# Two graph layers on one core: the hooks between the matmuls moved, merged and opened to ScalarE

## The chip, the cores and the metric

The kernel runs on one core of a Trainium2 chip. The metric is the device time of one execution in microseconds (us); lower is better. Everything is float32.

## The reference

128 graphs of 64 nodes with 768 features pass two layers, each followed by a residual and a layer norm. Cut to what matters:

```python
# layer 0, h = x
u = h @ h.T / sqrt(768);  p = softmax(u);  delta = p * adj
attn = delta / (sum(delta) + 1e-10)
ctx = upper(attn) @ (h @ Wl.T + bl) + diag(attn) * (h @ Ws.T + bs) + lower(attn) @ (h @ Wr.T + br)
x = layernorm(h + relu(layernorm(ctx) * gamma + beta))
# layer 1, 12 heads of 64
q, k, v = heads(x @ Wq + bq), heads(x @ Wk + bk), heads(x @ Wv + bv)
s = where(adj > 0, q @ k.T / 8 + abeta * adj, -9e15)
x = layernorm(x + softmax(s) @ v)
```

## The kernel before

**Blocks and periods.** The 8192 tokens are 16 blocks of 512 (8 graphs, four tiles `t` of 128 tokens). After a prologue that does layer 0 of block 0 and most of block 1's, the loop over `n` runs 16 periods. Period n holds, in this order of TensorE's large work: `left`, `right` and `own` (the three weight products wl, wr, ws of layer 0 for block m = n+1), `val` (the product wv of layer 1 for block n), and `qk[0]`, `qk[1]`, `qk[2]` (q and k of block n, one group of heads each). Period 0 has no `left`, `right` and `own`, and the last has no layer 0 at all, so 14 periods are whole. The attention of block p = n-1 is finished in `left` and `right` of period n.

**Seven products at 14 places.** Every large product is done by `seven` (L250) with seven block products instead of eight, in the order 1, 2, 6, 5, 7, 4, 3, each for two halves j. That makes 14 *places*, numbered 2k+j for the k-th product of the order. Products 1, 6, 7, 4 accumulate in the two PSUM tiles X[0], X[1], products 2, 5 and 3 use Y[0], Y[1]. Behind product 1, 6 and 7 `first` copies X with the bias to `u` (VectorE L297, or ScalarE L520 as `uqk` in the q/k products); `last` writes the outputs (L409 into `lr` for wl and wr, L391 into `o` for ws, L499 into `v` for wv, L528 into q and k). A later product can't go on in X or Y before those reads are done. In the trace one float32 matmul stands as two records, so a place of three matmuls is "x6".

**Hooks.** Small work is put ahead of a place by hand: `at(left, 4, f)` runs f ahead of place 4 of that stage (`hooks`, L259). The functions that the change moves:

- `turned_weights` (L572) transposes softmax weights by TensorE into the PSUM tile `ps_e` (pool `ps_tr`, two buffers, shared with `ps_a`), ScalarE copies to `eT`; `scores` (L533), `weighted` (L586) and `finish` (L611: layer norm and output of block p) are the rest of attention.
- `sides` (L372) transposes layer 0's attention through `ps_a` to `aT`; `context0` (L414) multiplies it with `lr` at the places of `val` (tile `ps_ctx`, pool `ps_mm` with two buffers) and puts the two norms, the affine step and the residual in the queue; the last step `norm` also stores x to DRAM as `x1d` (L447, by GpSimd's queue), because a block is loaded back in 32 x 32 squares:
- `squares` (L195) loads the tile `sq` (one buffer, 128-byte rows, four DMAs by ScalarE's queue, L201), from `x1d` for layer 1's input or from the input x for the next block's layer 0. `turned` (L205) transposes it on VectorE in six steps (L210) to `xT` or `hT`, and `combined` (L217) makes the sums S1, S2, S4 on GpSimd, four operations (L222 to L225). `begin1`, `turn1`, `sums1` are these three for layer 1, `begin`, `turn0`, `sums0` for layer 0, where `sums0` also runs `attention0` (matmuls `u`, L330).
- `loads` (L303) loads the plain tiles `xa` for the residual, by SyncE's queue, which also loads all weight pieces (pool `wst`, four buffers).

**Two queues of steps.** What VectorE and ScalarE do between is put by `later` in two lists, `urgent` and `lazy`. `step` (L119) runs behind every place and takes one item, from `urgent` first. An item marked `act` (an exponential or a square root on ScalarE) runs only where `act_free` is true and doesn't use up the step; a `GAP` leaves one step's room for the result. `settle(key)` (L130) runs all items of a kind at once. In q/k products `act_free` is false at most places:

```python
step(not taps_by_act or (j == 0 and i in (2, 5, 3)))
```

The loop runs under a manual schedule: each engine's instructions stand in the order in which this code issues them, and each engine goes through its own list in order. ScalarE's, SyncE's and GpSimd's DMAs stand in those lists too.

Of the kernel before, what the change touches and what calls it, by code (L numbers as in the profile page):

```python
# [11 lines left out]
F32 = mybir.dt.float32  # L12
AF = mybir.ActivationFunctionType
ALU = mybir.AluOpType
# [3 lines left out]
P = 128  # L18
# [5 lines left out]
T = 4  # L24
# [20 lines left out]
def gnn_two_layers(ctx: ExitStack, tc, x, adj, wl, bl, ws, bs, wr, br, gamma, beta,  # L45
# [204 lines left out]
    def seven(width, factors, first, last, hooks, taps_by_act=False):  # L250

        X, Y, u = {}, {}, {}
        for k, i in enumerate(ORDER):
            for j in range(2):
                for f in hooks.get(2 * k + j, ()):  # L259
                    f()  # L260
                if i == 1:
                    X[j] = ps_st.tile([P, 512], F32, tag="X", name="ps_X")
                if i in (2, 5):
                    Y[j] = ps_st.tile([P, 512], F32, tag="Y", name="ps_Y")
                ps = (X if i in (1, 6, 7, 4) else Y)[j][:, 0:width]
                fs = factors(i, j)
                for c, (a, b) in enumerate(fs):
                    nc.tensor.matmul(ps, lhsT=a, rhs=b, start=(c == 0 and i in (1, 2, 5)), stop=(c == len(fs) - 1),  # L268
                                     skip_group_check=True)
                if i == 1:  # L270
                    u[j, 1] = first(j, 0, ps)
                elif i == 2:
                    last(j, 0, 0, ps, u[j, 1])
                elif i == 6:
                    u[j, 2] = first(j, 1, ps)
                elif i == 7:
                    u[j, 3] = first(j, 1, ps)
                    last(j, 1, 1, Y[j][:, 0:width], u[j, 3])
                elif i == 4:
                    last(j, 1, 0, ps, None)  # L280
                elif i == 3:
                    last(j, 0, 1, ps, u[j, 2])
                step(not taps_by_act or (j == 0 and i in (2, 5, 3)))

    def by_tokens(nm, S, last, in_sbuf=None, hooks={}):

# [127 lines left out]
    def context0(n):  # L414

        blk = blocks[n]
        xa, o, dg = blk["xa"], blk["x"], blk["dg"]

        def part(t, h):
            cols = slice(h * HALF, (h + 1) * HALF)  # L420
            ps = ps_mm.tile([P, 512], F32, tag="mm", name="ps_ctx")
            for g in range(2):
                nc.tensor.matmul(ps[g * L : (g + 1) * L, 0:HALF], lhsT=blk["aT"][:, t, g * L : (g + 1) * L],  # L423
                                 rhs=blk["lr"][t][:, g, cols], start=True, stop=True)
            nc.vector.scalar_tensor_tensor(o[t][:, cols], o[t][:, cols], dg[:, t : t + 1], ps[:, 0:HALF],  # L425
                                           ALU.mult, ALU.add)
            if (t, h) == (T - 1, 1):
                rest()

        key = ("o", n)  # L430

        def affine(t, mean, rstd):
            nc.vector.scalar_tensor_tensor(o[t], o[t], mean, affine_of["gamma"], ALU.subtract, ALU.mult)

        def affine2(t, mean, rstd):
            nc.vector.scalar_tensor_tensor(o[t], o[t], rstd, affine_of["beta"], ALU.mult, ALU.add)

        def residual(t):
            nc.vector.scalar_tensor_tensor(o[t], o[t], 0.0, xa[t], ALU.max, ALU.add)

        squared = 0 < n < NBLK - 1
        blk["x_d"] = x_d = tc.dram_tile([NTOK, D], F32, name=f"x1d_{n}") if squared else None

        def norm(t, mean, rstd):
            nc.vector.tensor_scalar(o[t], o[t], mean, rstd, ALU.subtract, ALU.mult)  # L445
            if squared:
                nc.gpsimd.dma_start(out=x_d[t * P : (t + 1) * P, :], in_=o[t])  # L447

        def rest():
            for t, mr in enumerate(moments(key, o, 1e-12)):  # L450
                later(key, partial(affine, t, *mr), partial(affine2, t, *mr), partial(residual, t))
            for t, mr in enumerate(moments(key, o, 1e-5)):
                later(key, partial(norm, t, *mr))

        return [partial(part, t, h) for t in range(T) for h in range(2)]


    def transposed1(n):
# [110 lines left out]
              lambda: nc.vector.tensor_tensor(s8, s8, per_row(rz), ALU.mult), queue=urgent)  # L569
        blk[hg] = s  # L570

    def turned_weights(n, hg, t0, pool=None):  # L572

        blk = blocks[n]
        settle(("s", n, hg))
        e = blk[hg]
        if t0 == 0:
            blk["eT", hg] = (pool or l1_p).tile([P, T, 2, P], F32, tag="lr" if pool else "eT", name="eT")
        eT = blk["eT", hg]
        ps = ps_tr.tile([P, 4, P], F32, tag="tr", name="ps_e")  # L580
        for t in range(2):
            for c in range(2):
                nc.tensor.transpose(ps[:, 2 * t + c, :], e[:, t0 + t, c].rearrange("p r m -> p (r m)"), ident)
        nc.scalar.copy(eT[:, t0 : t0 + 2].rearrange("p t c i -> p (t c) i"), ps)

    def weighted(n, hg, tiles=range(T)):  # L586

# [95 lines left out]
    for n in range(NBLK):  # L683
# [4 lines left out]
        def at(hooks, place, f, *args):  # L688
            hooks.setdefault(place, []).append(partial(f, *args))

        def spread(hooks, place, fs):
            for k, f in enumerate(fs):
                at(hooks, place + k, f)
# [2 lines left out]
        last = n == NBLK - 1  # L696
        if p >= 0:
            one, two, three = (left, left, right) if not last else (qk[0], qk[1], qk[1])
            at(one, 2, turned_weights, p, 1, 0)
            at(one, 1 if not last else 2, scores, p, 2)  # L700
            at(one, 3, turned_weights, p, 1, 2)
            at(one, 5, weighted, p, 1)
            for k in range(2):
                at(two, 11 + k if not last else 1 + 2 * k, turned_weights, p, 2, 2 * k)
            at(two, 13 if not last else 5, weighted, p, 2)
            at(three, 0 if not last else 6, finish, p)

        if not last:
            if n > 0:
                if m + 1 < NBLK:  # L710
                    at(left, 4, edges, m + 1)
                at(right, 2, sides, m)
                sq1 = {}

                def begin1():
                    settle(("o", n))
                    blocks[n]["sq1"], sq1["fs"] = squares(blocks[n]["x_d"])

                at(right, 4, begin1)
                fetch = {}  # L720

                def begin2():
                    fetch["fs"] = loads(m)

                at(right, 8, begin2)
                for t in range(T):
                    at(right, 8 + t, lambda t=t: fetch["fs"][t]())
                for a in range(P // Q):
                    at(right, 4 + a, lambda a=a: sq1["fs"][a]())
                at(own, 0, settle, ("f", p))  # L730

                def turn1():
                    blocks[n]["xT"] = turned(("t1", n), blocks[n]["sq1"], f"xT_{n}")
                    later(("m", n), *mask(n), queue=urgent)

                at(own, 2, turn1)

                def sums1():
                    settle(("t1", n))
                    blocks[n]["S"] = combined(blocks[n]["xT"])  # L740

                at(own, 9, sums1)
                if m + 1 < NBLK:
                    sq = {}

                    def begin():
                        blocks[m + 1]["sq"], sq["fs"] = squares(x_b[m + 1])

                    at(own, 10, begin)
                    for a in range(P // Q):  # L750
                        at(own, 10 + a, lambda a=a: sq["fs"][a]())
                side_part(m, "l", None, left)
                side_part(m, "r", None, right)
                self_part(m, None, own)
            spread(val, 1, context0(m))
            if m + 1 < NBLK:

                def turn0():
                    blocks[m + 1]["hT"] = turned(("t", m + 1), blocks[m + 1]["sq"], f"hT_{m + 1}")

                at(val, 7, turn0)

                def sums0():
                    settle(("t", m + 1))
                    attention0(m + 1)

                at(qk[0], 2, sums0)

        if not last:
            values(n, val)  # L770
# [4 lines left out]
        at(qk[1], 2, scores, n, 0)  # L775
        at(qk[2], 2, scores, n, 1)
        if not last:
            for k in range(2):
                at(qk[2], 1 + 2 * k, turned_weights, n, 0, 2 * k)
            at(qk[2], 5, weighted, n, 0)  # L780
        for hg in range(NHG):
            projected(n, hg, qk[hg])
# [2 lines left out]

    for t0 in (0, 2):
        for hg in range(NHG):
            turned_weights(n, hg, t0, l0t if hg else None)
        for hg in range(NHG):
            weighted(n, hg, range(t0, t0 + 2))  # L790
            settle(("y", n, hg))
        finish(n, range(t0, t0 + 2))
        settle(("f", n))
# [31 lines left out]
```

## Time and profile before

| | |
|---|---|
| time, median of 3 runs | 3141.28 us (3139.05 to 3143.47) |
| the profiled execution | 3140.72 us, its span 3139.0 us |
| TensorE busy | 3022.5 us (96%) |
| VectorE, ScalarE, GpSimd busy | 2180.1, 398.3, 343.3 us |
| DMA | 541.20 MB, 172 GB/s over the span; the queue of `sq` moves 44.05 MB in 347568 packets |
| `left` of period 3 to `left` of period 4 | 711.07 to 903.64, 192.57 us |

How to read the views: a row of the timeline has the start in us, the duration, the engine, the line and operation, the tiles written and read, the shape, the count of merged records, and in brackets how long the engine stood idle before it and what released it. PE is TensorE, PEld its weight loads, DVE VectorE, ACT ScalarE, POOL GpSimd, SP SyncE; a "q" behind the name is the engine's sequencer, which issues DMAs. In the list of waits the columns are who waited for whom, us in total, times, and the longest.

### The profile page before, as it was taken

The page shows a single profiled execution, that of the slowest core. Times are in us where ns is not written, and L with a number is a line of the kernel's source. Part 1 is how long each engine was busy: PE and PEld are TensorE (multiplying, and loading weights), DVE is VectorE, ACT ScalarE, POOL GpSimd, SP SyncE. Part 2 cuts the span into 40 slices and gives each one's busy share as a digit, 9 for nine tenths or more (in the row PEclk, how much of TensorE's full clock was granted, in tenths as well). Part 3 has the DMA queues.
Part 4 walks back from the last instruction along what each step waited for, and adds up shares of the span by engine and source line. Part 5 has one row for each costly group of instructions (what it writes and reads, how often), then busy time and mean ns, then how long its engine had stood idle before and what let it go on. Part 6 is the DMA issues. An engine that isn't in the chain of part 4 may idle for free.

```text
span 3139.0 us, 45071 instructions
## 1 busy us (share of the span) xinstructions
PE 3022.5 (96%) x18144; PEld 2010.8 (64%) x18144; DVE 2180.1 (69%) x4163; ACT 398.3 (13%) x689; POOL 343.3 (11%) x317
## 2 busy tenths in 40 slices
PE   8899999999999999999999999999999999999997
PEld 5457657575674856758566585665757657575685
DVE  5747767677675866858667676676767767676756
ACT  0001102020020201102011020110201102020031
POOL 2321010100101001010100101001010010100010
PEclk9999999999999999999999999999999999999998
DMA  7663764937649475584755848568494764947343
GB/s 283 215 221 116 197 157 148 229 119 218 141 157 213 137 208 137 174 193 139 213 136 185 173 138 217 133 186 176 143 229 124 206 154 148 223 125 219 122 126 119
DMA packets 547791, 541.20 MB, mean 172 GB/s; under 512 B 372641, under 2 KB 452129, under 8 KB 547585
## 3 DMA queue, kind: packets, MB, share of 16 engines
q1 hardware_dynamic: 185424, 429.38, 43.9%
q10 hardware_dynamic: 347568, 44.05, 12.5%
q0 software_dynamic: 14592, 64.89, 5.5%
q8 instruction: 145, 2.38, 0.3%
q14 instruction: 62, 0.50, 0.1%
HBM read 473.37 MB, written 64.88 MB: 171 GB/s over the span
## 4 chain that ended last, share of the span: by engine, by line
issue 49%; PE 31%; DVE 8%; DMA 6%; POOL 4%; ACTq 2%; ACT 0%; POOLq 0%; SPq 0%; DVEq 0%
PE ps_X L268 15%; PE ps_Y L268 11%; DVE v L499 3%; PE ps_ctx L423 3%; DMA x1d<-o 3%; DVE hT L210 2%; ACTq L201 2%; DMA sq<-in_x_dram 1%; DVE u L297 1%; PE u L330 1%; POOL S L225 1%; POOL S L224 1%; POOL hT L223 1%; POOL x1d L447 1%; DMA sq<-x1d 1%
## 5 line engine op out<-in xcount | busy, mean ns | idle before, releaser
L268 PE MATMUL ps_X<-xT,wqk 128*128 128x256 f32 x1728 | 391.3, 379 | 0.0
L268 PEld LDWEIGHTS ps_X<-xT,wqk 128*128 128x128 f32 x1728 | 326.9, 190 | 47.0
L268 PE MATMUL ps_Y<-S,wqk 128*128 128x256 f32 x1152 | 264.3, 379 | 0.0
L268 PE MATMUL ps_X<-wr,hT 128*128 128x384 f32 x540 | 208.4, 542 | 53.5 <-DVE u L297 53.5
L409 DVE TENSOR_TENSOR lr<-ps_Y,u 64x384 f32<-64x384 f32 x384 | 213.2, 555 | 59.5 <-PE ps_Y L268 51.7
L268 PEld LDWEIGHTS ps_Y<-S,wqk 128*128 128x128 f32 x1152 | 218.9, 190 | 29.8
L520 ACT ACTIVATE uqk<-ps_X,bq 128x256 f32<-128x256 f32 x144 | 68.1, 473 | 1321.1 <-PE ps_X L268 1321.1
L268 PEld LDWEIGHTS ps_X<-wr,hT 128*128 128x128 f32 x540 | 113.1, 212 | 143.6 <-DVE u L297 64.9
L268 PE MATMUL ps_X<-wv,xT 128*128 128x384 f32 x576 | 200.2, 494 | 0.3
L238 DVE BATCH_NORM_STATS2 stats<-o 128x6 f32<-128x384 f32 x384 | 192.8, 543 | 1.4
L268 PE MATMUL ps_X<-ws,hT 128*128 128x384 f32 x540 | 184.7, 494 | 8.6 <-DMA ws<-d_s 5.4
L268 PE MATMUL ps_X<-wl,hT 128*128 128x384 f32 x540 | 188.3, 495 | 3.8 <-DVE std L243 2.7
L447 POOL DMA_DIRECT2D x1d<-o x56 | 30.5, 546 | 1333.2 <-DVE o L445 1318.1
L499 DVE TENSOR_TENSOR v<-ps_Y,u 64x192 f32<-64x192 f32 x384 | 136.4, 355 | 41.5 <-PE ps_Y L268 35.2
L268 PEld LDWEIGHTS ps_X<-wv,xT 128*128 128x128 f32 x576 | 105.4, 190 | 90.1 <-DVE u L297 17.4
L268 PEld LDWEIGHTS ps_X<-ws,hT 128*128 128x128 f32 x540 | 102.5, 192 | 84.6 <-DVE u L297 10.4
L528 DVE TENSOR_TENSOR q<-ps_Y,uqk 128x256 f32<-128x256 f32 x144 | 60.7, 421 | 133.2 <-ACT uqk L520 82.8
L268 PEld LDWEIGHTS ps_X<-wl,hT 128*128 128x128 f32 x540 | 101.7, 193 | 68.1 <-issue 4.4
L268 PE MATMUL ps_Y<-xT,wqk 128*128 128x256 f32 x576 | 140.2, 388 | 1.4 <-issue 1.4
L268 PE MATMUL ps_X<-S,wqk 128*128 128x256 f32 x576 | 136.7, 382 | 0.0
L268 PE MATMUL ps_Y<-wv,S 128*128 128x384 f32 x384 | 134.6, 494 | 0.0
L425 DVE SCALAR_TENSOR_TENSOR o<-o,dg,ps_ctx 128x384 f32<-128x384 f32 x128 | 78.5, 614 | 74.4 <-PE ps_ctx L423 73.3
(183 smaller groups left out, 4601.6 us busy)
## 6 DMA issues: line engine op xcount, KB each, us to landing
wqk<-qk_d SPq DMA_DIRECT2D x336, 384.0 KB, 3.0
wv<-d_v SPq DMA_DIRECT2D x64, 576.0 KB, 6.6
ws<-d_s SPq DMA_DIRECT2D x60, 576.0 KB, 6.3
wl<-d_l SPq DMA_DIRECT2D x60, 576.0 KB, 3.7
wr<-d_r SPq DMA_DIRECT2D x60, 576.0 KB, 4.0
wv<-in_L_gnn_Wv_dram SPq DMA_DIRECT2D x48, 576.0 KB, 4.2
ws<-in_L_gnn_W_self_dram SPq DMA_DIRECT2D x45, 576.0 KB, 4.8
wl<-in_L_gnn_W_left_dram SPq DMA_DIRECT2D x45, 576.0 KB, 3.9
```

What stands on the lines that cost most here:

```text
L201: nc.scalar.dma_start(out=sq[a * Q : (a + 1) * Q].rearrange("p s c i -> p (s c) i"), in_=by_group[a])
L210: nc.vector.transpose(xT[:, c, :].rearrange("p (j s) -> p s j", s=SQ), sq[:, :, c, :])
L223: nc.gpsimd.tensor_tensor(a21, a11, a21, ALU.subtract)
L238: nc.vector.bn_stats(stats[:, h, :], tiles[t][:, h * HALF : (h + 1) * HALF])
L268: nc.tensor.matmul(ps, lhsT=a, rhs=b, start=(c == 0 and i in (1, 2, 5)), stop=(c == len(fs) - 1), skip_group_check=True)
L409: nc.vector.tensor_tensor(lr[t][half * L : (half + 1) * L, g, cols], ps[rows], bias[nm][rows, cols] if part is None else part[rows], ALU.add)
L423: nc.tensor.matmul(ps[g * L : (g + 1) * L, 0:HALF], lhsT=blk["aT"][:, t, g * L : (g + 1) * L], rhs=blk["lr"][t][:, g, cols], start=True, s ...
L425: nc.vector.scalar_tensor_tensor(o[t][:, cols], o[t][:, cols], dg[:, t : t + 1], ps[:, 0:HALF], ALU.mult, ALU.add)
L447: nc.gpsimd.dma_start(out=x_d[t * P : (t + 1) * P, :], in_=o[t])
L499: nc.vector.tensor_tensor(v[r * L : (r + 1) * L, t, g, h * 3 : (h + 1) * 3, :], pairs(ps)[rows, r], add[rows, r], ALU.add)
L520: nc.scalar.activation(u, ps, AF.Identity, bias=bias["qk"[j]][:, c : c + 1])
L528: nc.vector.tensor_tensor(dst, ps, part, ALU.add)
```

## The change

- **Loads of layer 1's squares:** `begin1` and its four loads go from place 4 of `right` to place 10, so behind the square root of `finish` in ScalarE's list. `turn1` goes from place 2 of `own` to 4, `sums1` from 9 to 12. The next block's squares (`begin`) go from `own` 10 to `val` 0, `turn0` from `val` 7 to 8, `sums0` from `qk[0]` 2 to 4. The plain loads of x (`begin2`) go from `right` 8 to 11 to `own` 0 to 3. `sides` goes from `right` 2 to `left` 11.
- **Small work together:** `turned_weights` does both pairs of tiles at one place (three times a period), mostly beside `scores` or `sides`; `context0` does both halves of a tile at one place, so four places of `val` (1, 3, 5, 7) instead of eight. Small work then stands at 12 places per period instead of 22.
- **ScalarE's steps:** in q/k products an `act` item may run behind every place but two.

```diff
-                step(not taps_by_act or (j == 0 and i in (2, 5, 3)))
+                step(not taps_by_act or (i, j) not in ((5, 1), (7, 0)))
...
-        def part(t, h):
...
-            if (t, h) == (T - 1, 1):
+        def part(t):
+            for h in range(2):
+                cols = slice(h * HALF, (h + 1) * HALF)
+                ps = ps_mm.tile([P, 512], F32, tag="mm", name="ps_ctx")
+                for g in range(2):
+                    nc.tensor.matmul(ps[g * L : (g + 1) * L, 0:HALF], lhsT=blk["aT"][:, t, g * L : (g + 1) * L],
+                                     rhs=blk["lr"][t][:, g, cols], start=True, stop=True)
+                nc.vector.scalar_tensor_tensor(o[t][:, cols], o[t][:, cols], dg[:, t : t + 1], ps[:, 0:HALF],
+                                               ALU.mult, ALU.add)
+            if t == T - 1:
                 rest()
...
-        return [partial(part, t, h) for t in range(T) for h in range(2)]
+        return [partial(part, t) for t in range(T)]
...
-    def turned_weights(n, hg, t0, pool=None):
+    def turned_weights(n, hg, tiles=range(T), pool=None):
...
+        for t0 in tiles[::2]:
+            ps = ps_tr.tile([P, 4, P], F32, tag="tr", name="ps_e")
+            for t in range(2):
+                for c in range(2):
+                    nc.tensor.transpose(ps[:, 2 * t + c, :], e[:, t0 + t, c].rearrange("p r m -> p (r m)"), ident)
+            nc.scalar.copy(eT[:, t0 : t0 + 2].rearrange("p t c i -> p (t c) i"), ps)
...
-            at(one, 2, turned_weights, p, 1, 0)
             at(one, 1 if not last else 2, scores, p, 2)
-            at(one, 3, turned_weights, p, 1, 2)
+            at(one, 1 if not last else 2, turned_weights, p, 1)
             at(one, 5, weighted, p, 1)
-            for k in range(2):
-                at(two, 11 + k if not last else 1 + 2 * k, turned_weights, p, 2, 2 * k)
+            at(two, 11 if not last else 2, turned_weights, p, 2)
...
-                at(right, 2, sides, m)
+                at(left, 11, sides, m)
...
-                at(right, 4, begin1)
+                at(right, 10, begin1)
...
-                at(right, 8, begin2)
+                at(own, 0, begin2)
                 for t in range(T):
-                    at(right, 8 + t, lambda t=t: fetch["fs"][t]())
+                    at(own, t, lambda t=t: fetch["fs"][t]())
                 for a in range(P // Q):
-                    at(right, 4 + a, lambda a=a: sq1["fs"][a]())
+                    at(right, 10 + a, lambda a=a: sq1["fs"][a]())
...
-                at(own, 2, turn1)
+                at(own, 4, turn1)
...
-                at(own, 9, sums1)
+                at(own, 12, sums1)
...
-                    at(own, 10, begin)
+                    at(val, 0, begin)
                     for a in range(P // Q):
-                        at(own, 10 + a, lambda a=a: sq["fs"][a]())
+                        at(val, a, lambda a=a: sq["fs"][a]())
...
-            spread(val, 1, context0(m))
+            for t, f in enumerate(context0(m)):
+                at(val, 1 + 2 * t, f)
...
-                at(val, 7, turn0)
+                at(val, 8, turn0)
...
-                at(qk[0], 2, sums0)
+                at(qk[0], 4, sums0)
...
-            for k in range(2):
-                at(qk[2], 1 + 2 * k, turned_weights, n, 0, 2 * k)
+            at(qk[2], 2, turned_weights, n, 0)
```

More of the change, by code (lines that the diff above doesn't have):

```diff
@@ L417, in context0 @@
         xa, o, dg = blk["xa"], blk["x"], blk["dg"]
-        def part(t, h):
[L420 to L426, printed above, removed]
-            if (t, h) == (T - 1, 1):
+        def part(t):
[8 more added lines that the diff above has]
+            if t == T - 1:
                 rest()
@@ L576, in turned_weights @@
         e = blk[hg]
-        if t0 == 0:
+        if 0 in tiles:
             blk["eT", hg] = (pool or l1_p).tile([P, T, 2, P], F32, tag="lr" if pool else "eT", name="eT")
         eT = blk["eT", hg]
[L580 to L584, printed above, removed]
+        for t0 in tiles[::2]:
[4 more added lines that the diff above has]
+            nc.scalar.copy(eT[:, t0 : t0 + 2].rearrange("p t c i -> p (t c) i"), ps)
     def weighted(n, hg, tiles=range(T)):
@@ L787, in gnn_two_layers @@
         for hg in range(NHG):
-            turned_weights(n, hg, t0, l0t if hg else None)
+            turned_weights(n, hg, range(t0, t0 + 2), l0t if hg else None)
         for hg in range(NHG):
```

## The prediction

> **What bounds the kernel now.** I read the page's busy shares first, then the list of who waited for whom, then the timeline of one period (711.07 to 903.64 us, the one that starts layer 0 of block 4), TensorE alone and then all engines.
>
> ```profile
> PE 3022.5 (96%) x18144; PEld 2010.8 (64%) x18144; DVE 2180.1 (69%) x4163; ACT 398.3 (13%) x689; POOL 343.3 (11%) x317
> ```
>
> TensorE sets the time. Only what stops it, or what shortens its own work, counts. Its waits:
>
> ```profile
> PE ps_X L268 <- DVE u L297: 60.3, 21, 7.1
> PE u L330 <- DVE hT L210: 11.6, 14, 0.8
> ```
>
> Columns: total us, times, longest. The timeline shows where they fall (start, us, engine, line, operation; in brackets the idle time before it):
>
> ```profile
> 759.70 4.03 PE L268 MATMUL ps_X<-wr,hT 128*128 128x384 f32 x12
> 766.81 5.83 PE L268 MATMUL ps_X<-wr,hT 128*128 128x384 f32 x12 [3.08 <-DVE u L297]
> 772.48 4.03 PE L268 MATMUL ps_Y<-wr,S 128*128 128x384 f32 x12
> ...
> 791.83 5.97 PE L268 MATMUL ps_X<-ws,hT 128*128 128x384 f32 x18
> 799.17 2.20 PE L268 MATMUL ps_X<-ws,hT 128*128 128x384 f32 x6 [1.38 <-DVE u L297]
> 801.21 4.03 PE L268 MATMUL ps_Y<-ws,S 128*128 128x384 f32 x12
> ```
>
> Twelve records (two places) start 3.87 us apart when nothing disturbs, 1.935 a place. The four places from 759.70 to 772.48 should take 7.74 and take 12.78: 5.04 lost, of which 3.08 stand in brackets; the 12 records behind the wait are stretched to 5.67. The same four places in `right` over all 14 periods lose 82.8 us (3.9 to 9.4 each), the four in `own` 6.0. Why is `u` late?
>
> ```profile
> 758.00 0.17 DVE L243 TENSOR_SCALAR std<-mv 128x4 f32<-128x4 f32 x1
> 762.26 3.59 ACTq L201 DMA_DIRECT2D sq<-x1d  x2
> 765.89 0.20 ACT L246 ACTIVATE std<-std 128x4 f32<-128x4 f32 x1 [26.49 <-DMA ws<-in_L_gnn_W_self_dram]
> 766.13 0.18 DVE L247 RECIPROCAL rstd<-std 128x4 f32<-128x4 f32 x1 [7.50 <-ACT std L246]
> 766.23 0.53 DVE L297 TENSOR_TENSOR u<-ps_X,br 128x384 f32<-128x384 f32 x1
> ```
>
> The variance is ready at 758.17, but ScalarE's queue holds two loads of `sq` ahead of the square root, and those wait for the stores of `x1d`, the last issued at 755.91 and after. The reciprocal waits 7.50 us at the head of VectorE's queue, with `u` behind it and TensorE behind `u`.
>
> **What the Trainium skill says.** (1) "TensorE: Matmul & The Clock Gate", What's actually happening: the clock halves after about 3.4 us of idleness. The trace agrees in kind: the granted clock is 0.94 and 0.85 in the two 8 us windows after 760, so a wait costs more than its bracket: 82.8 lost for 53.5 waited in `right`. (2) "ScalarE: Activation LUTs", What ACT_TABLE_LOAD costs: 1.28 us plus a drain of 1.38 for each change of set. The trace has 1.28 (at 724.70, 843.59, 860.74, 872.39) with the activation right behind, so I use 1.28. (3) "DMA: Bandwidth & Descriptors", Queues, rings and completion order and Issuing engines are not separate DMA queues: all queues share 16 engines, which go round the queues packet by packet. The trace agrees: `sq`'s queue moves 3496 packets in 770 to 774, where the weights' queue stands still, and 1298 in 782 to 786 beside it.
>
> **The change part by part.**
>
> *Square roots ahead of loads.* In the changed program ScalarE's order is finish's root, then the four `sq` loads from `x1d`. ScalarE has nothing else there, so moving the hook six places later delays the loads by nothing but the root: they issue when `std` is ready (about 757.3, with `right` free of the 0.44 of `ps_a`; 762.26 before), since the `x1d` stores now all stand in `left`'s first places. Off the path goes the whole loss of `right`: −82.8.
>
> *Mask.* The loss in `own` (the wait at 799.17) is mask work (`m` and `off`, 1.81 and 1.89 us) queued ahead of `u`. `turn1` two places later puts the mask behind the last `u` of the stage; the next `u` is in `val`: −6.0. GpSimd's four combining operations (1.81 each) start when the last transpose is done, about 795, and end near 802; `val` reads the third at its place 4, about 808: nothing.
>
> *Layer-0 transposes and `u` (L330), one and two places later.* Here a stall doesn't go, it changes its place. VectorE's backlog at the end of `val` (places from 840.31 are qk[0]'s):
>
> ```profile
> 840.31 2.75 PE L268 MATMUL ps_X<-xT,wqk 128*128 128x256 f32 x12
> 842.06 1.46 DVE L499 TENSOR_TENSOR v<-ps_Y,u 64x192 f32<-64x192 f32 x4
> 844.60 1.46 DVE L499 TENSOR_TENSOR v<-ps_Y,u 64x192 f32<-64x192 f32 x4
> ```
>
> The last two `v` groups read the two accumulators Y that places 2 and 3 of qk[0] reuse, and end at 843.52 and 846.06. Before, the 4 us of `u` at place 2 hid that. With `u` at place 4 nothing does: place 2, due at 842.9, waits 0.7; place 3, due at 844.95, waits 1.2; by then `hT` is done and the old 0.83 is gone. The one period before that has no such `u` shows the wait:
>
> ```profile
> 2957.63 2.96 DVE L499 TENSOR_TENSOR v<-ps_Y,u 64x192 f32<-64x192 f32 x8
> 2959.20 3.07 PE L268 MATMUL ps_Y<-xT,wqk 128*128 128x256 f32 x12 [1.42 <-issue]
> ```
>
> So 14 × (0.7 + 1.2 − 0.83) = +15. `combined`, later too, is read in the next period: nothing.
>
> *Context, 8 places to 4.*
>
> ```profile
> 807.90 2.20 PE L268 MATMUL ps_X<-wv,xT 128*128 128x384 f32 x6
> 810.04 0.87 PE L423 MATMUL ps_ctx<-lr,aT 128*64 128x384 f32 x4
> 810.83 2.20 PE L268 MATMUL ps_Y<-wv,xT 128*128 128x384 f32 x6
> ```
>
> A place and its context take 2.93. The large work is 1.935, the two pairs at full rate 0.645 (a 384-wide record is 0.3225), so an interruption costs 0.2 (2.14 against 1.935) to 0.35. Four fewer in each of 15 periods: −12 to −21, I take −15. Both `ps_mm` buffers are used at one place; VectorE empties them in 1.3 us and the next pair comes 4.7 us later: no wait.
>
> *Transposed weights put together.* Four records of `ps_e` take 0.435, the large work after them 1.94: no cost of interruption, so no gain. At `left` 11, though, three `ps_tr` tiles meet in two buffers: the third waits for ScalarE's copy (0.58, ending 1.27 after its transposes began, where 0.87 are covered). Three in a row waited 0.24 at 3112.79. 14 × 0.24 to 0.4: +4.
>
> *ScalarE's steps.* Exponentials and roots may now go at 12 of 14 places in q/k instead of 3. The two excluded leave `uqk` free before the accumulator is used 1.3 us later. At worst, in qk[2], exponential, table and root (1.06 + 1.28 + 0.20) stand before `uqk`, but the exponential's input is ready about 4 us before that `uqk` is. Table loads stay 4 a period. TensorE: 0. It empties VectorE's lists sooner, which is what brings the `x1d` stores forward.
>
> *Loads of x for the next block*, on SyncE's queue, moved from the last wr pieces to the ws pieces: 4 × 384 KB now issue at about 756 to 764 instead of 744 to 752, beside the `sq` loads. No `ws` piece seems endangered: ws is needed 11 us after its issue and lands in 4.8 to 6.3. But the loads share engines with `sq`, and the last two `sq` loads now wait for the second and fourth `xa` to land. This is the one cost I can't read off. Before, `sq` landed 22.4 to 26 us after its first issue where VectorE waited for it:
>
> ```profile
> 786.08 1.05 DVE L210 STREAM_TRANSPOSE xT<-sq 128x512 f32<-128x512 f32 x1 [3.17 <-DMA ws<-d_s]
> ```
>
> (786.08 − 762.26 = 23.8; its releaser is named wrongly, it is the `sq` load.) Now: 757.3 + 23.4 + 1.57 MB at 330 GB/s (4.8) = 785.5. With 5 us no longer lost, `own` starts at 771.35 and its place 4 ends at 781; behind the awaited transpose stand a `u`, three transposes and the next `u` (1.03 + 0.54 + 3.06 + 0.54, about 5.4 with handover), which TensorE needs at place 10, 790.7. So `sq` may land at 785.3 without a stop. Bounds: nothing (it lands at 783, since `x1d`'s stores no longer run then and the writes of the output come earlier) to 4 us a period (788, stretched by the clock); I take 1.0 × 14 = +14.
>
> *Sum*, against the profiled execution (3140.7, its span 3139.0, 0.6 below the median 3141.3): −82.8 − 6.0 + 15 − 15 + 4 + 14 = −71. So about **3070**. Without the residual and with the larger context gain, 3043; with the residual at 4 us, the smaller gain and the dearer `ps_tr` wait, 3117.
>
> **The rivals.** *The loads take most back* (0.12): `sq` lands at 789, 3.7 us late, 1.4-fold with the clock: 5.2 × 14 = +73 instead of +14, 3129. For it: the DMA share over 762 to 786 is 0.99 to 1.35, and all queues are in use. Against it: the output writes (1.6 MB) of that window now begin some 5 us earlier.
> *Slower* (0.08): the same wait, in `own` at the first L210, grows past what was removed. The gain without it is 85, 6.1 a period; with the stretched clock it is eaten up when `sq` lands 5 us late, at 790 to 791, 33 us after issue. At 795: 9.7 × 1.2 × 14 = +163, so 3219. For it, the chained waits (`xa` lands, then the last `sq` load issues, itself up to 15.4 us to landing); against it, no load of the 14 that VectorE waited for took over 26.
> *The change doesn't do what it says* (0.06): the reciprocal was not what held `u`, and VectorE's backlog in `right` stops TensorE as well. Then −6 + 15 − 15 + 4 is left, 3139. Against it: VectorE stood idle for the 7.50 us.
>
> **How the numbers follow.** Main case 0.74: 3070, with 3043 to 3117. The range is that with a margin below and part of the first rival: 3040 to 3120. Faster by over 0.2% (about what a measurement of this kernel can tell from no change): main case and first rival, 0.86. Slower 0.09 and within 0.2% 0.05, the last rival split between them.
>
> **What would show it.** Right: no bracket at the wr places, the reciprocal's wait under 1 us, two short waits at the first `ps_Y` of qk[0] and none of L330, a context place of 8 records in about 1.4 us, periods of some 187 us instead of 192.5. Wrong: a bracket at the ws places with VectorE's L210 waiting behind a DMA for more than 6 us (the residual), waits of TensorE on `ws`, or `u` still late in `right`.

## Result and profile after

The changed kernel is slower by 0.3%: median 3155.44 us (3142.75 to 3166.15, 20 runs) beside 3145.15 us (3132.27 to 3153.66, 20 runs) of the kernel before in the same comparison, ratio 1.0031 with a 95% interval of 1.0018 to 1.0044. I had forecast 3070. The profiled execution took 3156.40 us with a span of 3154.7, so 15.7 more than the 3139.0 of before.

The busy shares on the page of the changed kernel:

```profile
PE 3002.0 (95%) x18144; PEld 2020.2 (64%) x18144; DVE 2220.3 (70%) x4163; ACT 392.6 (12%) x689; POOL 344.3 (11%) x317
```

TensorE was busy 20 us less and still later done. Its list of waits (who waited for whom, total us, times, longest):

```profile
PE ps_X L268 <- DVE u L297: 83.6, 19, 9.3
PE ps_Y L268 <- DVE v L500: 15.0, 14, 1.1
PE ps_Y L268 <- PE ps_X L268: 7.6, 14, 0.6
...
PE ps_a L378 <- ACT eT L586: 4.1, 14, 0.3
```

The wait for `u` was to go, and is longer than the 60.3 of before. It is not the same wait. The period shown for before starts here at 713.78 us. TensorE's timeline through its `right` and `own`:

```profile
762.88 7.90 PE L268 MATMUL ps_X<-wr,hT 128*128 128x384 f32 x24
770.62 4.03 PE L268 MATMUL ps_Y<-wr,S 128*128 128x384 f32 x12
...
789.97 2.10 PE L268 MATMUL ps_X<-ws,hT 128*128 128x384 f32 x6
798.97 8.18 PE L268 MATMUL ps_X<-ws,hT 128*128 128x384 f32 x18 [6.91 <-DVE u L297]
806.99 4.03 PE L268 MATMUL ps_Y<-ws,S 128*128 128x384 f32 x12
```

In `right` the four places from 762.88 to 770.62 now take 7.74: nothing is lost. In `own` the same four places take 17.02, and 9.28 are lost: 6.91 in brackets, and 18 records that take 8.18 where before took 5.97. Over the 14 periods `right` loses 0.0 (82.8 before) and `own` 111.3 (6.0 before; 2.4 to 12.0 a period). The wait has changed its stage. What `u` waits for stands in VectorE's rows of the same timeline:

```profile
760.05 0.17 DVE L243 TENSOR_SCALAR std<-mv 128x4 f32<-128x4 f32 x1
760.12 0.55 DVE L297 TENSOR_TENSOR u<-ps_X,br 128x384 f32<-128x384 f32 x1
760.59 0.17 DVE L247 RECIPROCAL rstd<-std 128x4 f32<-128x4 f32 x1
...
784.36 0.56 DVE L297 TENSOR_TENSOR u<-ps_X,bs 128x384 f32<-128x384 f32 x1 [1.38 <-PE ps_X L268]
797.50 1.04 DVE L210 STREAM_TRANSPOSE xT<-sq 128x512 f32<-128x512 f32 x1 [12.58 <-DMA wv<-in_L_gnn_Wv_dram]
798.39 0.53 DVE L297 TENSOR_TENSOR u<-ps_X,bs 128x384 f32<-128x384 f32 x1
```

and in ScalarE's:

```profile
760.25 0.20 ACT L246 ACTIVATE std<-std 128x4 f32<-128x4 f32 x1 [18.71 <-DVE std L243]
760.54 25.73 ACTq L201 DMA_DIRECT2D sq<-x1d  x4
```

The reciprocal no longer waits: the root is ahead of the loads. But the loads are behind the root. Their data are there 37.0 us after the first issue (760.54 to 797.50), VectorE waits 12.58 us for them at its first transpose of `own`, and `u` is queued behind that transpose. (The releaser in brackets is wrong again.) The costliest groups of the changed kernel (busy us, mean ns, then the idle time ahead) say the same for all periods:

```profile
L210 DVE STREAM_TRANSPOSE xT<-sq 128x512 f32<-128x512 f32 x84 | 81.8, 1022 | 158.0 <-DMA sq<-x1d 131.2 <-DMA wv<-in_L_gnn_Wv_dram 26.8
L268 PE MATMUL ps_X<-ws,hT 128*128 128x384 f32 x540 | 211.7, 547 | 85.6 <-DVE u L297 80.6 <-DMA ws<-d_s 5.0
```

80.6 us waited cost 111.3. In the table by windows (us, TensorE busy, granted clock, DMA share, GB/s) the 8 us with the wait run at a clock of 0.57:

```profile
796.00:804.00 8.00, 5.03 (x9) 0.57 0.03 9
```

Why do 1.57 MB of squares take 37 us? In the view of the DMA queues (packets, MB, share of the 16 engines) `sq` is q10; q1 is SyncE's queue (weights and `xa`), q0 GpSimd's (stores). In the microsecond from 764 only `sq` moves (packets overlap in this view, so a share can pass 100%):

```profile
q10 hardware_dynamic: 1344, 0.17, 154.6%
```

In the one from 777 all three do:

```profile
q1 hardware_dynamic: 48, 0.22, 52.3%
q0 software_dynamic: 48, 0.20, 49.1%
q10 hardware_dynamic: 47, 0.01, 3.8%
```

Alone, `sq` moves 1344 packets in a microsecond. With both other queues full each of the three moves about as many packets as the others (262, 223 and 250 from 775 to 780), and one of `sq` is 128 bytes where the others' are over 4 KB on average. Equal counts are not the whole of it: from 767 to 769 `sq` moved nothing at all beside SyncE's queue, though its second load had been issued at 763.42:

```profile
q1 hardware_dynamic: 375, 0.69, 106.0%
```

From 766 to 781 `sq` passed 1815 of its 12352 packets. In the period of before, where they needed 21 us (763 to 784, 588 per us), 1815 would take 3.1. By this count some 12 us were lost in that stretch; this landing (37.0) is 13.2 longer than that of before (23.8). What filled the other queues: SyncE's rows of the timeline, with the loads of x that the change put here,

```profile
759.63 0.48 SPq L727 DMA_DIRECT2D xa<-in_x_dram  x1
763.50 0.96 SPq L727 DMA_DIRECT2D xa<-in_x_dram  x2
767.42 0.46 SPq L727 DMA_DIRECT2D xa<-in_x_dram  x1
770.81 11.93 SPq L292 DMA_DIRECT2D ws<-d_s  x4
```

and GpSimd's, with the stores of the output:

```profile
767.72 0.54 POOL L618 DMA_DIRECT2D out_dram<-o  x1 [39.01 <-DVE o L617]
...
773.92 0.54 POOL L618 DMA_DIRECT2D out_dram<-o  x1 [1.33 <-DVE o L617]
```

A second delay stands in ScalarE's list, the chained waits of the prediction. A load of `sq` can wait with its issue for a semaphore that it shares with a load of SyncE. The third begins here:

```profile
770.28 11.59 ACTq L201 DMA_DIRECT2D sq<-x1d  x1
```

At 770.26 the second load of `xa` landed, which raises that semaphore. In all 14 periods the third load so waits for an `xa` load, with ScalarE's list idle for 5.1 to 6.1 us; before, the last three loads follow one another within 0.4 us. How much of the 37.0 us is due to this wait and how much to the shared engines, these traces don't separate.

The other two places that I had named, the merged context (`val`) and `qk[0]`, on TensorE's timeline:

```profile
810.86 2.10 PE L268 MATMUL ps_X<-wv,xT 128*128 128x384 f32 x6
812.88 1.51 PE L424 MATMUL ps_ctx<-lr,aT 128*64 128x384 f32 x8
814.33 2.20 PE L268 MATMUL ps_X<-wv,xT 128*128 128x384 f32 x6
816.36 2.10 PE L268 MATMUL ps_Y<-wv,xT 128*128 128x384 f32 x6
...
848.01 1.53 PE L268 MATMUL ps_Y<-xT,wqk 128*128 128x256 f32 x6 [0.55 <-PE ps_X L268]
850.61 1.53 PE L268 MATMUL ps_Y<-xT,wqk 128*128 128x256 f32 x6 [1.07 <-DVE v L500]
```

### The profile page after: what moved, and what is told of

Its sections match the earlier page's. It is cut to its first block, busy times and chain, and to the rows that moved or that the text cites. A ratio compares the mean times of both kernels' runs of the same rounds, so it can differ in the third digit from the quotient of the medians.

```text
span 3154.7 us, 45047 instructions
## 1 busy us (share of the span) xinstructions
PE 3002.0 (95%) x18144; PEld 2020.2 (64%) x18144; DVE 2220.3 (70%) x4163; ACT 392.6 (12%) x689; POOL 344.3 (11%) x317
## 4 chain that ended last, share of the span: by engine, by line
PE 67%; DMA 12%; DVE 8%; issue 7%; ACTq 4%; POOL 1%; ACT 0%; SPq 0%; DVEq 0%; POOLq 0%
PE ps_X L268 33%; PE ps_Y L268 26%; DMA sq<-x1d 6%; ACTq L201 4%; DVE v L500 4%; PE ps_ctx L424 3%; DMA xa<-in_x_dram 3%; DVE hT L210 2%; PE sc L547 1%; PE ps_y L599 1%; PE u L330 1%; PE ps_e L585 1%; DMA wqk<-qk_d 1%; DVE u L297 1%; DMA b_l<-in_L_gnn_W_left_dram 1%
## 5 line engine op out<-in xcount | busy, mean ns | idle before, releaser
L268 PE MATMUL ps_X<-ws,hT 128*128 128x384 f32 x540 | 211.7, 547 | 85.6 <-DVE u L297 80.6
L268 PEld LDWEIGHTS ps_X<-ws,hT 128*128 128x128 f32 x540 | 114.1, 215 | 177.4 <-DVE u L297 95.2
L210 DVE STREAM_TRANSPOSE xT<-sq 128x512 f32<-128x512 f32 x84 | 81.8, 1022 | 158.0 <-DMA sq<-x1d 131.2
L268 PE MATMUL ps_X<-wr,hT 128*128 128x384 f32 x540 | 179.1, 486 | 0.0
L268 PEld LDWEIGHTS ps_X<-wr,hT 128*128 128x128 f32 x540 | 102.5, 190 | 71.3
L268 PEld LDWEIGHTS ps_Y<-xT,wqk 128*128 128x128 f32 x576 | 104.3, 190 | 46.4 <-issue 20.9
L297 DVE TENSOR_TENSOR u<-ps_X,bl 128x384 f32<-128x384 f32 x96 | 53.4, 557 | 109.6 <-PE ps_X L268 109.0
```

Source lines behind the costliest of these rows:

```text
L210: nc.vector.transpose(xT[:, c, :].rearrange("p (j s) -> p s j", s=SQ), sq[:, :, c, :])
L297: nc.vector.tensor_tensor(u, ps, bias[nm][:, b * HALF : (b + 1) * HALF], ALU.add)
```

## The experiments

**Theory.** Opening more places to ScalarE's steps alone frees `right`, since layer 0's norms and the stores of `x1d` finish early. Putting the loads behind the root then gives up an earlier start and sends them among the loads of x and the stores. **Rival A:** it is the 1.57 MB of `xa` alone that delays the squares. **Rival B:** the place of the hook (right 10) is what counts, not what stands ahead of it. Times are medians; the ratio is to the kernel before in the same comparison; "lost" is the sum over 14 periods at the four places, as above.

| run | time, us | ratio (95%) | lost in `right` / `own` |
|---|---|---|---|
| after | 3155.44 | 1.0031 (1.0018 to 1.0044) | 0.0 / 111.3 |
| e1_xa_back | 3094.0 | 0.9832 (0.9795 to 0.9868) | 0.0 / 49.1 |
| e2_before_xa_own | 3193.7 | 1.0146 (1.0121 to 1.0171) | 136.8 / 5.3 |
| e3_before_begin1_r10 | 3202.12 | 1.0176 (1.0137 to 1.0216) | 0.0 / 17.0, and a new wait |
| e4_squares_r0 | 3047.75 | 0.9684 (0.966 to 0.9707) | 0.0 / 0.0 |
| e5_half_stores | 3064.2 | 0.9732 (0.9702 to 0.9763) | 0.0 / 26.0 |
| e6_u_back | 3034.1 | 0.9645 (0.9628 to 0.9662) | 0.0 / 0.0 |
| e7_spread | 3010.98 | 0.9572 (0.9554 to 0.9589) | 0.0 / 0.0 |
| e8_before_context | 3125.46 | 0.9921 (0.9898 to 0.9945) | 88.3 / 7.1 |
| e9_before_steps | 3054.09 | 0.9711 (0.9692 to 0.973) | 0.0 / 2.9 |
| e10_after_r4 | 3046.61 | 0.9668 (0.9643 to 0.9692) | 0.0 / 0.0 |
| e11_after_r6 | 3163.33 | 1.0051 (1.0036 to 1.0065) | 0.0 / 121.2 |
| e12_eighth_stores | 3056.03 | 0.9693 (0.9666 to 0.972) | 0.0 / 12.1 |

**e1_xa_back:** the changed kernel with the loads of x where they were.

```diff
-                at(own, 0, begin2)
+                at(right, 8, begin2)
...
-                    at(own, t, lambda t=t: fetch["fs"][t]())
+                    at(right, 8 + t, lambda t=t: fetch["fs"][t]())
```

> The changed kernel with the plain loads of x (xa) back at places 8 to 11 of right. Theory 'x loads starve the squares': xa is in by the time the squares' loads start, sq lands about 24 us after its first issue instead of 37, the loss in own falls from 111 us to under 15, time about 3050 to 3065. Rival 'outputs starve them' (the writes of finish, which now begin earlier and share the same engines): sq still lands 30 us or more after issue, the loss stays above 60 us, time above 3100.

62 of the 111 us go, 49.1 stay, between what I had put down for the theory and for its rival. From first issue to first transpose the squares still take 27.0 to 36.4 us, 31.8 on average, against 35.7 after the change and 23.4 before:

```profile
749.27 21.74 ACTq L201 DMA_DIRECT2D sq<-x1d  x4
...
781.35 1.03 DVE L210 STREAM_TRANSPOSE xT<-sq 128x512 f32<-128x512 f32 x1 [7.71 <-DMA sq<-x1d]
```

So rival A is right for somewhat more than half of the loss, and not for the rest. The run takes away both the bytes of `xa` beside the squares and the third load's wait for `xa`; it doesn't separate them. In its place the fourth load now waits in all 14 periods, for 4.0 to 7.0 us, until a piece of `ws` has landed.

**e2_before_xa_own:** the same edit the other way round, in the kernel before.

> The kernel before with one part of the change alone: xa at places 0 to 3 of own. Theory 'x loads starve the squares': sq lands some 8 to 12 us later than before, the wait in right stays (loss about 83 us) and a wait in own of 4 to 8 us a period comes on top: 3190 to 3250. Rival 'outputs starve them': no change beyond 10 us.

The time is in the range, but by luck: neither of the two effects in my sum came. The loads take 25.0 us on average from first issue to first transpose, 23.4 before, not 8 to 12 more, and `own` loses nothing more. Instead `right` loses more, because two of the loads stand ahead of the root there and the root is later still. The last store of `x1d`, which these loads wait for, lands 8.45 us after its issue (5.54 before), and the issue of the two takes 6.35 us (3.59 before). ScalarE's and VectorE's rows of the timeline (of one period, as in all that follow):

```profile
780.95 0.20 ACT L246 ACTIVATE std<-std 128x4 f32<-128x4 f32 x1 [32.17 <-issue]
...
781.18 0.18 DVE L247 RECIPROCAL rstd<-std 128x4 f32<-128x4 f32 x1 [13.18 <-ACT std L246]
```

**e3_before_begin1_r10:** the kernel before with the squares' loads behind the root, alone.

```diff
-                at(right, 4, begin1)
+                at(right, 10, begin1)
...
-                    at(right, 4 + a, lambda a=a: sq1["fs"][a]())
+                    at(right, 10 + a, lambda a=a: sq1["fs"][a]())
```

> The kernel before with one part of the change alone: the squares' loads at places 10 to 13 of right, so behind the square root; turn1 stays at place 2 of own. Theory 'the root behind the loads is what held u': the loss in right goes from 82.8 us to under 5. The last x1d stores then come by the lazy queue, the loads start at about the old time and land about as late as before against a period that no longer stops in right, so a wait in own of 3 to 6 us a period takes its place: 3110 to 3160. Rival 'the backlog of VectorE in right holds u as well': the loss in right stays above 40 us.

The root is no longer held, `right` loses nothing, and the kernel is 1.8% slower, beyond the range I gave. This moving alone turns one wait into another, longer one (the whole of `own` loses 156.7 us), and the loads take 27.6 us on average, 23.4 before; ScalarE's and VectorE's rows of its timeline:

```profile
774.12 18.07 ACTq L201 DMA_DIRECT2D sq<-x1d  x4
...
802.09 1.03 DVE L210 STREAM_TRANSPOSE xT<-sq 128x512 f32<-128x512 f32 x1 [14.74 <-DMA sq<-x1d]
```

and in its list of TensorE's waits a new one, `o` queued behind these transposes:

```profile
PE ps_Y L268 <- DVE o L391: 109.6, 14, 12.7
```

**e4_squares_r0:** the changed kernel with these loads ahead of the root, from place 0 of `right`.

```diff
-                at(right, 10, begin1)
+                at(right, 0, begin1)
...
-                    at(right, 10 + a, lambda a=a: sq1["fs"][a]())
+                    at(right, a, lambda a=a: sq1["fs"][a]())
```

> The changed kernel with the squares' loads of layer 1 at places 0 to 3 of right, four places ahead of the square root instead of six behind it; xa stays in own. The x1d stores are in by then. Theory 'only the start of the loads against their traffic matters': they issue at 740 to 755 on the scale of the changed kernel, land before 775, and both losses are 0: 3040 to 3055. Rival 'any load ahead of the root delays it': the reciprocal waits and a loss in right of 40 us or more comes back, above 3085.

Both losses are gone, every period takes about 185.96 us (194.04 on average after, 192.46 before). The root stands behind the loads as before the change, and its reciprocal waits only 1.75 us in the period shown and 3.2 at most (6.6 to 11.6 before).

**e5_half_stores** and **e12_eighth_stores:** e1 with shorter stores of the output, 384 and 96 columns of 768.

```diff
-            nc.gpsimd.dma_start(out=out_t[n, t], in_=xt[t])
+            nc.gpsimd.dma_start(out=out_t[n, t, :, 0:HALF], in_=xt[t][:, 0:HALF])   # e12: 0:96
```

> e1 (x loads back in right) with the output stores of finish cut to the first 384 of 768 columns, so half of the output is left out; all else is as in e1. It asks why e1's squares still take 27 to 36 us from first issue to the first transpose where the kernel before took 22 to 26. Theory 'output stores share the engines with them': the loads land 3 to 5 us earlier than in e1, the loss in own falls from 49 us to under 15, 3050 to 3065. Rival 'the weights, which TensorE now asks for without a pause': the loss stays above 35 us, above 3080.

> e1 with the output stores of finish cut to 96 of 768 columns, so seven eighths of the output are left out. Half of the stores took the loss in own from 49 to 26 us. Theory 'output stores are the rest of the starvation': the loss falls under 10 us, 3045 to 3055. Rival 'the weights, asked for without a pause, are the rest': the loss stays near 20 us, 3065.

The loss falls with the stores: 49.1, 26.0, 12.1; the first step lies between my two values, the second just misses the range. The squares take 31.8, 29.4 and 28.3 us on average. The stores are most of the loss that the loads of x leave over. Some 12 us a run are not explained by either. Two things are left to see in e12: the fourth load waits for a piece of `ws` in all periods, for 4.5 to 6.9 us, and SyncE's queue of weights can still hold up the squares (170 packets against 10 of `sq` from 765 to 767, with no other queue at work). No run took the weights away.

**e9_before_steps:** the kernel before with the one line on ScalarE's steps.

```diff
-                step(not taps_by_act or (j == 0 and i in (2, 5, 3)))
+                step(not taps_by_act or (i, j) not in ((5, 1), (7, 0)))
```

> The kernel before with one part of the change alone: ScalarE's steps at 12 of 14 places of q/k. Theory 'the x1d stores come forward': the norms of layer 0 finish in left's first places, so the squares' loads, still ahead of the root in ScalarE's list, issue before right begins and no longer hold the root: the loss in right falls from 83 us to under 15, 3055 to 3070. Rival 'loads ahead of the root always delay it': the loss in right stays above 50 us, above 3110.

This line alone makes the kernel 2.9% faster. The loss in `right` is gone without any load being moved: the last store of `x1d` is issued at 710.60, so the two loads ahead of the root are issued by 730.1, long before it is wanted. GpSimd's and ScalarE's rows of the timeline:

```profile
710.60 0.54 POOL L447 DMA_DIRECT2D x1d<-o  x1 [9.88 <-DVE o L445]
...
724.68 5.42 ACTq L201 DMA_DIRECT2D sq<-x1d  x2
...
742.62 0.21 ACT L246 ACTIVATE std<-std 128x4 f32<-128x4 f32 x1 [11.21 <-DVE std L243]
```

The root waits for its input (`std`), not for a place in the queue.

**e10_after_r4** and **e11_after_r6:** the changed kernel with the loads from place 4 (where they were) and from place 6.

```diff
-                at(right, 10, begin1)
+                at(right, 4, begin1)     # e11: 6
...
-                    at(right, 10 + a, lambda a=a: sq1["fs"][a]())
+                    at(right, 4 + a, lambda a=a: sq1["fs"][a]())
```

> The changed kernel with one part undone: the squares' loads of layer 1 back at places 4 to 7 of right, so one of the four ahead of the square root in ScalarE's list. xa stays in own. Theory 'the start of the loads decides, and the first loads ahead of the root start early': the first load issues in left, the rest behind the root at about the time of the changed kernel; between e4 and the changed kernel, about 3085 to 3125, with a loss in own of 40 to 80 us. Rival 'one load more or less doesn't matter': 3150 as the changed kernel.

> The changed kernel with the squares' loads at places 6 to 9 of right instead of 10 to 13: still behind the root in ScalarE's list. Theory 'the place counts only through what stands ahead in the list': no change against the changed kernel, 3145 to 3160, loss in own 100 to 115 us. Rival 'earlier is better in itself': a gain of 20 us or more.

Two places apart, 117 us apart. From place 4 two of the four loads stand ahead of the root and start 26.1 us after the period's start (693.4 there), against 46.8 in the changed kernel; the other two follow the root. ScalarE's rows of e10:

```profile
719.47 2.67 ACTq L201 DMA_DIRECT2D sq<-x1d  x2
...
739.88 0.20 ACT L246 ACTIVATE std<-std 128x4 f32<-128x4 f32 x1 [16.43 <-DVE std L243]
739.89 5.11 ACTq L201 DMA_DIRECT2D sq<-x1d  x2
```

From place 6 all four stand behind it, and it is as slow as from place 10, even a little slower than I expected. Rival B falls: between these places only what stands ahead in ScalarE's list counts. My number for e10 was a miss by some 40 us, since I counted one load ahead of the root; half the packets early is enough. In this kernel the later pair meets the same crowded stretch, and `own` loses nothing: some six thousand of the packets are in by then.

**e8_before_context:** the kernel before with the context at four places.

> The kernel before with one part of the change alone: context0 at four places of val instead of eight. Theory: an interruption of the large products costs 0.35 us (the changed kernel's trace has two places and a merged context in 5.50 us, the kernel before two places and two contexts in 5.86), so 15 x 4 x 0.36 = 22 us less than before, ratio 0.993. Rival: the gain is eaten by the wait in right, ratio 1.000.

20 us less: the merged context is a gain by itself.

**e6_u_back:** e4 with layer 0's transposes and `u` where they were.

```diff
-                at(val, 8, turn0)
+                at(val, 7, turn0)
...
-                at(qk[0], 4, sums0)
+                at(qk[0], 2, sums0)
```

> e4 (squares at right 0) with turn0 and sums0 back at val 7 and qk[0] 2. Theory 'the stall only moved': the waits of 0.55 and 1.07 us at the first ps_Y of qk[0] go, the 0.83 in front of u (L330) comes back: 14 x 0.8 = 11 us less than e4, 3036. Rival 'the later place is better': not under e4.

14 us less than e4: the two waits at `ps_Y` go, the 0.8 at L330 comes back.

**e7_spread:** e4 with the mask in a place of its own and VectorE's transposes earlier.

```diff
-                at(left, 11, sides, m)
+                at(right, 2, sides, m)
...
-                    later(("m", n), *mask(n), queue=urgent)
-                at(own, 4, turn1)
+                at(own, 1, turn1)
+                at(own, 10, lambda: later(("m", n), *mask(n), queue=urgent))
...
-                at(val, 8, turn0)
+                at(val, 5, turn0)
...
-                at(qk[0], 4, sums0)
+                at(qk[0], 2, sums0)
```

> e4 with turn1 at own 1, its mask apart at own 10, turn0 at val 5, sums0 at qk[0] 2, sides at right 2. The squares of layer 1 are in long before own 1 in e4, so the buffer sq comes free earlier, the next block's squares land earlier, and VectorE's backlog at the end of val shrinks. Theory: the waits in front of u and at ps_Y of qk[0] and at ps_a all go, 14 x (1.62 + 0.29) = 27 us under e4, about 3021. Rival 'the next squares are not in by val 5': VectorE waits there, and TensorE with it by 1 us a period or more, not under 3040.

3010.98 us, the fastest of all and 4.3% under the kernel before; it is 10 us less than I expected, and since the run moves five things at once it doesn't say which of them gave that. The periods take 183.35 us, and no wait of TensorE is left that comes back each period; the longest in its list are those of the ends of the program:

```profile
PE ps_x L192 <- DMA xa<-in_x_dram: 6.2, 2, 5.6
PE ps_X L268 <- DMA ws<-d_s: 4.9, 1, 4.9
```

## Why the prediction was wrong

By its own sum:

| term | predicted | measured |
|---|---|---|
| loss in `right` | −82.8 | −82.8 |
| mask and residual in `own` | −6.0 + 14 | +105.3 (6.0 to 111.3) |
| first places of `qk[0]` | +15 | +11 (15.0 + 7.6 for the 11.6 at L330) |
| context | −15 (−12 to −21) | −22 (two places with their context 5.50, 810.86 to 816.36, for 2 × 2.93 before: 0.36 × 4 × 15) |
| `ps_a` behind ScalarE's copy | +4 | +4.1 |
| sum | −71 | +16; the spans differ by 15.7 |

**Right:** the reading of the wait in `right`, and that it would go; the two short waits in `qk[0]` with their sizes; the context (−20 in e8, alone); `ps_a`; and the start of the loads, taken as 757.3 in before's period, 46.2 after its start, measured 46.8.

**Wrong, the step that failed:** the landing, "757.3 + 23.4 + 1.57 MB at 330 GB/s (4.8)", so 28.2 us after issue. Measured were 37.0 in the same period, 31.0 to 39.4 over all and 35.7 on average. The term that was mis-sized is the 23.4, not the 4.8: with `xa` back in its old place (e1) the loads still take 31.8, so `xa` adds 3.9 and the base is 8.4 too short. I took the duration from before as a property of the loads, but it was measured in periods in which TensorE stood still for some us, and SyncE's weights paused with it (a piece needs one of the four buffers of `wst`, which TensorE frees). Before, SyncE issues two pieces of `ws` 3.87 us apart and the next only 8.91 us later:

```profile
759.89 4.24 SPq L292 DMA_DIRECT2D ws<-in_L_gnn_W_self_dram  x2
772.67 11.93 SPq L292 DMA_DIRECT2D ws<-d_s  x4
```

The prediction has that gap in its own figures, the 3496 packets of `sq` in 770 to 774 "where the weights' queue stands still", and didn't ask what becomes of it when TensorE no longer waits. In the changed kernel the pieces come every 3.87 us. e3, in which `right` doesn't stop either, shows 27.6. What makes up the 8.4 is not shown in full: cutting the stores by seven eighths (e12) takes 3.5 off, but before had the stores too, and the fourth load's wait for `ws`, which before didn't have, was not tested alone.

The Trainium skill's page "DMA: Bandwidth & Descriptors", Queues, rings and completion order, which I had cited for the turns packet by packet, says that an engine changes queues only at the end of a packet. The trace agrees where all three queues are full (48, 48 and 47 packets in one microsecond), and for a queue of 128-byte packets that means 3.8% of the engines; it doesn't account for the two microseconds without any, and whether the trace's packets are the page's isn't shown.

The bound of 4 us a period for the residual was too small: it cost 8.0 on average (111.3 / 14, as the mask's 6.0 are gone in e4).

**Not priced at all:** the start that was given up. I wrote that moving the hook "delays the loads by nothing but the root". That is so against before, where the stores of `x1d` held them. But by my own next words those stores "now all stand in `left`'s first places", so the loads could have started some 20 us earlier in the period, away from `xa`, the stores and the weights, and the root they would have stood ahead of would not have been held. e4 has this with all four loads and e10 with two; e10 takes 3046.61, the moving behind the root costs 109 us. So one part of the change (the steps, e9: 3054.09) had already done what another part (the loads) was for, and the other part then took it away. That part helps neither kernel: alone it costs 1.8% (e3).

**The rivals:** the one called "Slower" names what happened, the same wait in `own` past what was removed, decided by a landing of 33 us or more after issue. I gave it 0.08 and argued against it with "no load of the 14 that VectorE waited for took over 26", though those were measured without `xa` in the queue and beside a TensorE that waited. Of what it gave as reasons for, the chained wait of the third load came as written. The size of the loss lay between my two values: at 37 us after issue the period lost 9.28. "Doesn't do what it says" was excluded rightly. One sum of the prediction doesn't come out: without the residual and with the larger context gain its own terms give 3050, not 3043.

**How the parts add up:** from e9 (3054.09), the context −20, `qk[0]` +11, `ps_a` +4 and the mask −2.9 give 3046; e10 and e4 measured 3046.61 and 3047.75. With the squares late, the 111.3 of `own` on top would be 3158, and after is 3155.44. The split of the 111.3 is 62 for the loads of x (e1) and 37 for the stores (e1 against e12), taken away in this order; the rest is open.

## What to carry to other kernels

Before moving an operation to clear a queue, ask whether another part of the same change already empties what it waits for; if so, the moving only costs its early start. A DMA's duration read beside a stalled engine may hold only with that stall: ask which queues paused with it, and whether they still will. Give a DMA of small packets a stretch in which the other queues pause, or start half of it early, as e10 does. And when two hook positions differ, look at what each puts ahead in the engine's own list before counting places.

## What was not expected of the hardware

- A queue of 128-byte packets fell to 3.8% of the engines beside two queues of packets of over 4 KB on average, all three with equal counts; alone it had moved 1344 packets in a microsecond.
- ScalarE's list was held by the issue of four such loads for 25.73 us, 18.0 of them the issues themselves (the third alone from 770.28 for 11.59, where the first took 0.57) and the rest waits between them. Anything behind such loads in its list waits with them: of the 13.18 us that a reciprocal waits in e2, 6.35 are the issue of two.
- The issue of a load on ScalarE's queue waited for the landing of a load on SyncE's (770.28 behind 770.26).
- The clock makes a wait dearer here too: 80.6 us waited in `own` cost 111.3, a factor of 1.38.
